# Blocks of normed rows transposed by VectorE and placed through memory, in a two-layer transformer kernel on one core

## The chip, the cores and the metric

The kernel runs on one core of a Trainium2 chip. The core has a matrix engine (TensorE, PE in the profile), a vector engine (VectorE, DVE), an activation engine (ScalarE, ACT), a general engine (GpSimd, POOL), an engine that mostly issues transfers (SyncE, SP), and 16 DMA engines that move data between the core's memory (SBUF) and device memory. Each engine runs its own instructions strictly in order and waits on semaphores for what other engines have still to deliver. The metric is the device time of one execution in microseconds (us): 2072.71 us, the median of three runs (2072.71, 2074.32 and 2067.70).

## What is computed

Two transformer layers on 4 × 512 tokens of 512 channels, in 32-bit floats. Cut to what matters here:

```python
x  = hidden_states                                  # 4 x 512 x 512
xn = layernorm(x)
x  = x + ttt_attention(xn) + ternary_ffn(xn)        # layer 0
xn = layernorm(x)
x  = x + latent_attention(xn) + moe_ffn(xn)         # layer 1

# ttt_attention: 32 heads of 16; per head a recurrence over 32 mini-batches of 16 tokens
Z1 = xk @ W1 + b1;  grad = fused_ln_l2_backward(Z1, xv - xk)
W1 = W1 - (eta * xk).T @ grad;  b1 = b1 - sum(eta * grad)
# ternary_ffn: silu(xn @ gate.T * gs) * (xn @ up.T * us) @ down.T * ds, inner size 1408
# latent_attention: c_kv = xn @ W_DKV + b, c_q = xn @ W_DQ + b, then 16 heads of 128
# moe_ffn: token g*4+e goes to expert e (fixed); silu(gate) * up @ down, inner size 512
```

What counts for the change is `xn`, twice. Layernorm is done with a token on each partition and its 512 channels along the free axis. The matmuls that use `xn` need it the other way round: a channel on each partition and tokens along the free axis. So each block of normed rows must be transposed.

## The kernel before

The first layer works in eight chunks of 256 tokens (`NCHUNK`, `CW`; 64 tokens of each of the four sequences). A chunk has two halves `u` of 128 rows. A loop over the 32 mini-batches issues the recurrence, which is a chain of short operations, and between its parts calls `fill(us)`. That draws work from a list of generators: the generator `between(ch)` yields, piece by piece with a cost estimate each, the products of the feed-forward net of chunk `ch` (`gate_up`, line 465, eleven times, then `down`, line 483), the transposition, keys, token rates and queries of chunk `ch + 1`, and `finish(ch - 1)`, which norms the recurrence's output, multiplies by `wo`, stores the layer's result to `yd` and norms it again for layer 1. At the end of `between(ch)` stands `norm_rows(ch + 2)`: loads of `x` and its layernorm. The order of each engine's instructions is made from this program order by the framework's scheduler; loads and stores of this stage are issued on SP (`nc.sync`), but for the last chunk's stores, which are on ScalarE's queue.

The rows are transposed in `transposed(src)` (line 144): four TensorE products with the identity, each turning 128 × 128, into one PSUM buffer from the two-buffer pool `pj`. For `x`, `norm_turn` copies the result to `xT` on ScalarE (line 157). `xT` holds 128 channels × 4 channel blocks × 256 tokens and is what `gate_up` and the key, value and query products read. For layer 1's rows (`x1`), `finish` copies it on ScalarE (line 603), tokens regrouped by expert (token index mod 4), to `xs` and stores that in device memory as `xe_d`, 256 KB for a half in 128 runs of 2 KB (line 604). The last two chunks keep the copy in SBUF too. In the last chunk's `between`, `latent_rows` loads chunks 0 to 5 of `xe_d` back, and `latents` (line 627) makes the latent projections `lat_d` from them. These are evicted from PSUM by VectorE and ScalarE in turn, in four operations for each projection, one for each sequence.

The mixture of experts follows (lines 899 to 1078). POOL issues the load of the first expert's gate weights `gu_0` (2 MB, line 924) and 14 loads of `xe` (line 928); SP issues the last two (through `fetch`). `xe` holds layer 1's rows as 128 channels × 16 halves × 4 channel blocks × 4 experts × 32 tokens. `tokens(e, c, h)` (line 940) takes expert `e`'s tokens from it: runs of 32 numbers. The experts' first product is done by Strassen's scheme: `right_sums` (line 944) forms four sums of token blocks, `t_ops`, on VectorE, and `left_sums` those of the weights, `s_ops`. Ahead of this stage, at line 833, POOL sets a 128 × 128 tile `ones` to 1; only the last product for the bias `bo`, in the attention stage, reads it. Its memory is reused from the first layer's stage.

The attention stage over 16 heads and four sequences comes last (lines 1084 to 1372). It already transposes its probabilities on VectorE in 32 × 32 blocks (line 1163) and places the blocks with 64 KB transfers on SP (line 1194).

Of the kernel before, what the change touches and what calls it, by code (L numbers as in the profile page):

```python
# [18 lines left out]
P = 128  # L19
# [36 lines left out]
def trunk_kernel(ctx: ExitStack, tc: tile.TileContext, a: dict, out: bass.AP):  # L56
# [12 lines left out]
    nc.vector.memset(eps_ln, LN_EPS)  # L69
    dram = ctx.enter_context(tc.tile_pool(name="dram", bufs=1, space=bass.MemoryType.DRAM))  # L70
    yd = dram.tile([B, L, HS], F32, tag="yd", name="yd")
    xe_d = dram.tile([2 * NCHUNK, P, NC, E, 32], F32, tag="xe_d", name="xe_d")
    lat_d = dram.tile([1 + QC // P, P, B, NCHUNK, CT], F32, tag="lat_d", name="lat_d")
    bo = const.tile([P, HS], F32, tag="bo", name="bo")

# [30 lines left out]
    with ExitStack() as px:  # L106
# [34 lines left out]
        def transposed(src):  # L141
# [2 lines left out]
                nc.tensor.transpose(pt[:, c, :], src[:, c * P : (c + 1) * P], ident)  # L144
            return pt

        def norm_rows(ch):
            for u in range(2):
                xt = wk.tile([P, HS], F32, tag="xt", name=f"xt{ch}_{u}", bufs=4)
                load_rows(xt, a["x"], ch, u)  # L150
                row_norm(xt, xt, f"{ch}_{u}")
                xns[ch, u] = xt

        def norm_turn(ch):
            xTs[ch] = wk.tile([P, NC, CW], F32, tag="xT", name=f"xT{ch}", bufs=3)
            for u in range(2):
                nc.scalar.copy(xTs[ch][:, :, u * P : (u + 1) * P], transposed(xns.pop((ch, u))))
                yield 0.6

        norm_rows(0)  # L160

# [69 lines left out]
        lrb_s = one.tile([P, NS, 4], F32, tag="lrb_s", name="lrb_s")  # L231
        nc.vector.tensor_copy(lrb_s, lrb[:, :P].rearrange("p (al r) -> p r al", r=32)[:, :NS, :])

        for _ in norm_turn(0):
            pass


        rows_d = [dram.tile([CH, NS, K, B, RW], F32, tag=f"rows{ch}", name=f"rows{ch}") for ch in range(NCHUNK)]
# [13 lines left out]
        def keys(ch):  # L252
            return features(ch, wk_w, k1, "k1", 2)
# [291 lines left out]
        def finish(ch):  # L545
            store = nc.sync if ch + 1 < NCHUNK else nc.scalar
            zb = zbs.pop(ch)
            sq = wk.tile([P, NC, CW], F32, tag="pn_sq", name=f"pn_sq_{ch}", bufs=1)
            nc.scalar.activation(sq, zb, AF.Square)
            for j in range(2):  # L550
                pv = psum()
                mm(pv, bones, sq[:, 2 * j : 2 * j + 2].rearrange("p c t -> p (c t)"))
                rs = wk.tile([P, 2, CW], F32, tag="pn_rs", name=f"pn_rs_{ch}_{j}", bufs=1)
                nc.scalar.activation(rs.rearrange("p c t -> p (c t)"), pv, AF.Sqrt, bias=eps_ttt, scale=1.0 / HD)
                for c in range(2):
                    be = 2 * j + c

                    tc.keep_in_program_order(nc.vector.reciprocal(rs[:, c], rs[:, c]))
                    nc.vector.scalar_tensor_tensor(
                        zb[:, be], zb[:, be], gamma_ch[:, be : be + 1], rs[:, c], ALU.mult, ALU.mult  # L560
                    )
            nc.vector.tensor_add(zb, zb, q1[ch])
            yield 1.72
            pm = psum()[:, :CW]
            mm(pm, onesd, over_blocks(sq, zb))

            for be in range(NC):
                nc.vector.scalar_tensor_tensor(
                    zb[:, be], zb[:, be], beta_ch[:, be : be + 1], pm, ALU.add, ALU.subtract
                )  # L570
            nc.scalar.activation(sq, zb, AF.Square)
            over_blocks(sq, sq)
            yield 0.43
            pt = psum()
            rt = wk.tile([P, 2], F32, tag="pn_rt", name=f"pn_rt_{ch}")
            for u in range(2):
                mm(pt[:, u : u + 1], sq[:, 0, u * P : (u + 1) * P], onesd[:, :1])
            nc.scalar.activation(rt, pt[:, :2], AF.Sqrt, bias=eps_ttt, scale=1.0)
            nc.vector.reciprocal(rt, rt)
            for u in range(2):  # L580
                po = psum()
                for be in range(NC):
                    mm(po, zb[:, be, u * P : (u + 1) * P], wo[:, be, :], be == 0, be == NC - 1)
                t = yf.pop((ch, u))
                nc.vector.scalar_tensor_tensor(t, po, rt[:, u : u + 1], t, ALU.mult, ALU.add)
                for b2 in range(2):
                    store.dma_start(
                        out=yd[2 * u + b2, ch * CT : (ch + 1) * CT, :], in_=t[b2 * CT : (b2 + 1) * CT, :]
                    )

                xt = wk.tile([P, HS], F32, tag="xt", name=f"x1_{ch}_{u}", bufs=4)
                row_norm(xt, t, f"1_{ch}_{u}")
                xns[ch, u] = xt
                yield 4.4
            if ch >= NCHUNK - 2:
                t = wk.tile([P, NC, CW], F32, tag="xT", name=f"xl_{ch}", bufs=3)
                part = parts[ch] = t.rearrange("p c w -> p (c w)").rearrange("p (u c e x) -> p u c e x", u=2, c=NC, e=E)
            for u in range(2):
                if ch >= NCHUNK - 2:
                    xs = part[:, u]  # L600
                else:
                    xs = wk.tile([P, NC, E, 32], F32, tag="xs", name=f"xs_{ch}_{u}", bufs=3)
                nc.scalar.copy(xs, transposed(xns.pop((ch, u))).rearrange("p c (j e) -> p c e j", e=E))
                store.dma_start(out=xe_d[2 * ch + u], in_=xs)
                yield 0.6


# [12 lines left out]
                lw.extend(t[:, :, i * P : (i + 1) * P] for i in range(n // P))  # L620

        def latent_rows(k):
            t = parts[2 * k, 2 * k + 1] = one.tile([P, 4, NC, E, 32], F32, tag=("wk", "wv", "wq")[k], name=f"xl_{k}")
            for i in range(4):
                nc.sync.dma_start(out=t[:, i], in_=xe_d[4 * k + i])

        def latents(key):

            part = parts.pop(key)
            ks = key if isinstance(key, tuple) else (key,)  # L630
            n = len(ks)
            for m, w in enumerate(lw):
                pl = psum()[:, : n * CW]
                for c in range(NC):
                    mm(pl, w[:, c, :], part[:, :, c], c == 0, c == NC - 1)
                st = wk.tile([P, 512], F32, tag="xs", name=f"lat_{ks[0]}_{m}", bufs=3)
                view = pl.rearrange("p (k u e b j) -> p k u e b j", k=n, u=2, e=E, b=2)
                to = st[:, : n * CW].rearrange("p (b k e j) -> p b k e j", b=B, k=n, e=E)
                for b in range(B):
                    part_b = view[:, :, b // 2, :, b % 2]  # L640
                    if m % 2:
                        nc.vector.tensor_scalar(to[:, b], part_b, lat_b[:, m : m + 1], None, ALU.add)
                    else:
                        nc.scalar.activation(to[:, b], part_b, AF.Identity, bias=lat_b[:, m : m + 1], scale=1.0)
                nc.scalar.dma_start(
                    out=lat_d[m][:, :, ks[0] : ks[0] + n], in_=to.rearrange("p b k e j -> p b k (e j)")
                )
                yield 1.72 * n

# [6 lines left out]
        def between(ch):  # L656

            fin = finish(ch - 1) if ch > 0 else iter(())
            if ch + 1 == NCHUNK:
                latent_operands()  # L660
            for i in range(NI):
# [6 lines left out]
                yield from finish_constants()  # L668
            nxt = iter(())
            if ch + 1 < NCHUNK:  # L670
                nxt = chain(
                    norm_turn(ch + 1), keys(ch + 1), token_tile(ch + 1, 0), token_tile(ch + 1, 1), queries(ch + 1)
                )
            else:
                yield from fin
            for u in range(2):
# [153 lines left out]
    buv = lat.tile([P, H], F32, tag="b_UV", name="b_UV")  # L830
    bo_part = lat.tile([P, HS], F32, tag="bo_part", name="bo_part")
    ones = lat.tile([P, P], F32, tag="ones", name="ones")
    nc.gpsimd.memset(ones, 1.0)
    ups = ["uk"] + [f"uq{i}" for i in range(QC // P)]

    def batch_latents(hg, b):
# [62 lines left out]
    with ExitStack() as px:  # L899
# [22 lines left out]

        gu = gate_w[0]
        nc.gpsimd.dma_start(out=gu, in_=a["gu"][0].rearrange("(c p) o -> p c o", p=P))
        xe = wg.tile([P, 2 * NCHUNK, NC, E, 32], F32, tag="xe", name="xe")
        for k in range(2 * NCHUNK):
            if k < 2 * NCHUNK - 2:
                nc.gpsimd.dma_start(out=xe[:, k], in_=xe_d[k])
            else:
                fetch(out=xe[:, k], in_=xe_d[k])  # L930
        ws = {0: gu, 1: gates(1)}
        dns = {0: downs(0)}

# [5 lines left out]

        def tokens(e, c, h):  # L940

            return xe[:, NCHUNK * h : NCHUNK * (h + 1), 2 * c : 2 * c + 2, e, :].rearrange("p k c j -> p c k j")

        def right_sums(e):
            t1, t2, t3, t4 = (t_ops[:, n].rearrange("p c (k j) -> p c k j", k=NCHUNK) for n in range(4))
            b22 = tokens(e, 1, 1)
            nc.vector.tensor_sub(t1, tokens(e, 0, 1), tokens(e, 0, 0))
            nc.vector.tensor_sub(t2, b22, t1)
            nc.vector.tensor_sub(t3, b22, tokens(e, 0, 1))
            nc.vector.tensor_sub(t4, tokens(e, 1, 0), t2)  # L950

        def left_sums(gu, i):

# [84 lines left out]
        right_sums(0)  # L1038
        for e in range(E):
            if e == 1:  # L1040
                nc.sync.dma_start(out=wqr, in_=a["W_QR"])
                nc.sync.dma_start(out=wkr, in_=a["W_KR"])
                buv16 = wk.tile([H, D], F32, tag="sg", name="buv16")
# [426 lines left out]
```

## Time and profile before

| | |
|---|---|
| median of three runs | 2072.71 us |
| lowest, highest | 2067.70, 2074.32 us |
| profiled execution | 2068.84 us |
| its span (first to last instruction) | 2067.1 us |
| mean TensorE clock granted in it | 0.988 |
| first layer's recurrence and products | about 40 to 981 us |
| mixture of experts | about 988 to 1165 us |
| attention stage | about 1165 to 2067 us |
| instructions in the trace | 30725 |
| DMA moved | 271.94 MB in 341254 packets |

A profile shows one execution. "Busy" is time in which an engine worked on an instruction; the rest is waiting. A row of the timeline or of the list of groups names engine, line, operation, output and inputs with their shapes; "x4" counts instructions, and brackets hold the time for which the engine stood idle just before and what ended that wait. A product of 32-bit floats leaves two records in the trace, a transposition through the identity one. Durations of products overlap, so the time that a sequence takes is read from the starts, not from the sum of durations.

### The profile page before, as it was taken

What the parts mean: (1) busy time and instruction counts of PE and PEld (TensorE: products, weight loads), DVE (VectorE), ACT (ScalarE), POOL (GpSimd) and SP (SyncE); (2) the same over time, 40 slices, a digit from 0 to 9 for tenths busy, and PEclk for the clock granted to TensorE, in tenths of its full rate; (3) what the DMA queues carried; (4) which work ended last, traced back from release to release, by engine and by line L of the source; (5) the groups of instructions that cost most, each with busy time, mean ns of one, the idle gap of its engine ahead of it and who ended that gap; (6) DMA issues with size and microseconds to landing.
All of it is one profiled execution on the core that took longest, in us unless ns stands there. A gap on an engine that the chain in (4) does not pass through costs nothing.

```text
span 2067.1 us, 30725 instructions
## 1 busy us (share of the span) xinstructions
PE 1983.4 (96%) x10486; PEld 1255.6 (61%) x10486; DVE 1302.3 (63%) x2722; ACT 866.2 (42%) x1763; POOL 587.5 (28%) x635
## 2 busy tenths in 40 slices
PE   8998999899999999998699999999999999999998
PEld 6776676767667776745577435555555555555554
DVE  5444667475755674744454487777777777777772
ACT  2233343333343443421122265555555555555552
POOL 5232333333332333311000222233223232354220
PEclk9999999999999999999899999999999999999999
DMA  6756566656464656643831144344444443433332
GB/s 164 205 141 181 136 190 158 173 144 178 115 186 126 161 168 170 198 127 122 286 107 57 48 112 118 96 109 109 107 98 110 106 107 87 109 86 95 96 92 83
DMA packets 341254, 271.94 MB, mean 132 GB/s; under 512 B 104299, under 2 KB 262188, under 8 KB 340460
## 3 DMA queue, kind: packets, MB, share of 16 engines
q1 hardware_dynamic: 326112, 255.41, 46.0%
q0 software_dynamic: 3488, 9.27, 1.4%
q10 hardware_dynamic: 11500, 5.32, 0.9%
q8 instruction: 84, 1.38, 0.3%
q14 instruction: 70, 0.57, 0.1%
HBM read 174.18 MB, written 34.87 MB: 101 GB/s over the span
## 4 chain that ended last, share of the span: by engine, by line
PE 46%; SPq 2%; DVE 2%; ACT 1%; DMA 1%; issue 0%; DVEq 0%; ACTq 0%
PE pc L1202 9%; PE sc L1134 9%; PE pq L1124 7%; PE px L1245 5%; PE p L1245 4%; PE epg L966 3%; PE epo L1029 3%; PE pk L1116 2%; SPq L1194 2%; PE epu L966 1%; PE po L1302 1%; PE pw L865 1%; PE pvo L883 1%; ACT prob L1139 1%; DVE tt L1163 0%
## 5 line engine op out<-in xcount | busy, mean ns | idle before, releaser
L1139 ACT ACTIVATE prob<-sc,mx 128x512 f32<-128x512 f32 x256 | 174.3, 683 | 157.6 <-DVE mx L1136 152.7
L1134 PE MATMUL sc<-kT,qT 96*128 96x512 f32 x512 | 230.9, 593 | 0.9 <-ACT prob L1139 0.6
L1202 PE MATMUL pc<-prT,lv 128*128 128x512 f32 x496 | 224.8, 596 | 3.7 <-DMA prT<-tt 3.7
L1163 DVE STREAM_TRANSPOSE tt<-prob 128x512 f32<-128x512 f32 x252 | 173.1, 706 | 56.0 <-ACT prob L1144 44.5
L1109 POOL TENSOR_TENSOR kT<-t_k,t_k 32x512 f32<-32x512 f32 x64 | 80.6, 1259 | 407.7 <-PE pq L1124 225.4
L117 PE MATMUL pf<-xT,wg 128*128 128x256 f32 x704 | 175.7, 392 | 12.5 <-DVE hid L478 6.8
L1144 ACT ACTIVATE prob<-prob,sm 128x512 f32<-128x512 f32 x256 | 176.3, 713 | 0.0
L1124 PE MATMUL pq<-cq,uq 128*128 128x512 f32 x384 | 175.3, 592 | 0.6 <-DVE t_k L1105 0.6
L117 PE MATMUL pf<-xT,wu 128*128 128x256 f32 x704 | 171.7, 388 | 1.6 <-DMA wu<-in_wu 1.6
L1134 PEld LDWEIGHTS sc<-kT,qT 96*128 96x128 f32 x512 | 96.7, 190 | 124.9 <-issue 120.1
L1136 DVE TENSOR_REDUCE mx<-sc 128x1 f32<-128x512 f32 x256 | 168.1, 677 | 5.8 <-PE sc L1134 3.8
L117 PE MATMUL pd<-wd,hid 128*128 128x512 f32 x352 | 165.3, 599 | 0.4 <-DMA wd<-in_wd 0.2
L117 PEld LDWEIGHTS pf<-xT,wg 128*128 128x128 f32 x704 | 133.5, 194 | 39.3 <-DVE hid L478 9.8
L1202 PEld LDWEIGHTS pc<-prT,lv 128*128 128x128 f32 x496 | 94.8, 191 | 99.4 <-issue 96.4
L117 PEld LDWEIGHTS pf<-xT,wu 128*128 128x128 f32 x704 | 137.4, 196 | 21.8 <-DMA wu<-in_wu 1.8
L478 DVE SCALAR_TENSOR_TENSOR hid<-pf,us,sg 128x256 f32<-128x256 f32 x88 | 41.8, 476 | 145.9 <-ACT sg L477 145.1
L1124 PEld LDWEIGHTS pq<-cq,uq 128*128 128x128 f32 x384 | 72.8, 190 | 92.8 <-issue 83.6
L314 POOL TENSOR_SCALAR sk<-k,m 128x256 f32<-128x256 f32 x64 | 61.0, 964 | 202.8 <-PE pz L117 189.6
L421 POOL TENSOR_SCALAR gh<-grad,m 128x256 f32<-128x256 f32 x64 | 62.3, 983 | 152.8 <-DVE grad L390 145.2
L117 PEld LDWEIGHTS pd<-wd,hid 128*128 128x128 f32 x352 | 63.6, 190 | 58.7 <-issue 44.6
L477 ACT ACTIVATE sg<-pf,gs 128x256 f32<-128x256 f32 x88 | 41.5, 473 | 135.1 <-PE pf L117 134.7
L1109 POOL TENSOR_TENSOR qT<-t_q,t_q 32x512 f32<-32x512 f32 x64 | 80.7, 1260 | 56.9 <-DVE t_q L1105 56.8
(295 smaller groups left out, 3503.9 us busy)
## 6 DMA issues: line engine op xcount, KB each, us to landing
prT<-tt SPq DMA_DIRECT2D x1008, 64.0 KB, 2.0
wd<-in_wd SPq DMA_DIRECT2D x176, 256.0 KB, 3.0
wg<-in_wg SPq DMA_DIRECT2D x88, 256.0 KB, 3.0
wu<-in_wu SPq DMA_DIRECT2D x88, 256.0 KB, 3.2
cq<-lat_d SPq DMA_DIRECT2D x48, 256.0 KB, 3.9
rows<-rows SPq DMA_DIRECT2D x128, 66.0 KB, 2.2
kv<-rows SPq DMA_DIRECT2D x32, 264.0 KB, 4.3
gu<-in_gu SPq DMA_DIRECT2D x3, 2048.0 KB, 7.9
```

The costliest lines, as they stand in the source:

```text
L117: nc.tensor.matmul(out, lhsT=lhsT, rhs=rhs, start=start, stop=stop, skip_group_check=True)
L421: nc.gpsimd.tensor_scalar_mul(gh[:, :, h, :], g, m2[:, h : h + 1])
L966: nc.tensor.matmul(ps, lhsT=w[:, c, :], rhs=x[:, c], start=start and c == 0, stop=c == 1, skip_group_check=True)
L1109: nc.gpsimd.tensor_sub(t[RD:mid, :], t1[RD:mid, :], t2[RD:mid, :])
L1124: nc.tensor.matmul(pq, lhsT=w[f"uq{i}"][:, h, :], rhs=cqs[hg, b][:, i, :], start=(i == 0), stop=(i == nq - 1))
L1134: pin(nc.tensor.matmul(ps, lhsT=qT[:KQ, i * P : (i + 1) * P], rhs=kT[:KQ, :], start=True, stop=True))
L1136: pin(nc.vector.tensor_reduce(mx, ps, AX.X, ALU.max, negate=True))
L1139: pin(nc.scalar.activation(pr, ps, AF.Exp, bias=mx, scale=1.0, accum_out=sm))
L1144: pin(nc.scalar.mul(pr, pr, sm))
L1163: nc.vector.transpose(out=tt[:, :, :, i, :], in_=pr.rearrange("p (kb e j) -> p kb e j", e=2, j=K))
L1202: pin(nc.tensor.matmul(pc, lhsT=lv[:, b, k, :], rhs=prT[:, k, :], start=(k == 0), stop=(k == E - 1)))
L1245: nc.tensor.matmul(ps[:, q, :], lhsT=a[:, k, q * P : (q + 1) * P], rhs=w[:, k, :], start=start and k == 0 and q == 0, stop=k == 1, skip_gr ...
```

## The change

Normed rows are transposed by VectorE, except those of chunk 0 of `x` and of chunks 6 and 7 of `x1`. `nc.vector.transpose` on 128 × 512 turns each 32 × 32 block in place within its 32 partitions. The new `turned_out` then writes the tile to device memory with four stores on SP, one for each group of 32 partitions, 32 rows × 16 blocks × 128 bytes (64 KB), so that the blocks come to stand where a full transpose has them. For `x` it writes to the new `x_d[ch]` at the end of `norm_rows`; `norm_turn` is then one load of `xT` (512 KB, runs of 1 KB), at the start of `between(ch)` for chunk `ch + 1`, and no longer a pair of pieces among its work. For `x1` it writes `xe_d` in `finish`, right after the norm; the expert order within a block of 32 tokens comes from the write pattern of the VectorE operation.

`xe_d` has a new layout: per half 16 blocks × 32 channels × 4 token groups × 32 tokens. All its loads go through `by_channel`, which gives runs of 512 bytes. So expert `e`'s tokens in `xe` come in runs of eight numbers; `tokens` is changed to that, and `right_sums` works in eight operations of 256 columns instead of four of 512. The evictions of the latents go by chunk and half row instead of by sequence. The setting of `ones` moves from line 833, ahead of POOL's loads of the mixture of experts, to the second expert's turn.

```diff
-    xe_d = dram.tile([2 * NCHUNK, P, NC, E, 32], F32, tag="xe_d", name="xe_d")
+    xe_d = dram.tile([2 * NCHUNK, 4 * NC, 32, 4, 32], F32, tag="xe_d", name="xe_d")
+    def by_channel(blocks):
+        return blocks.rearrange("(c q) r t x -> (q r) c (t x)", q=4)
...
+        x_d = [dram.tile([4 * NC, 32, 8, 32], F32, tag=f"x{ch}", name=f"x{ch}") for ch in range(NCHUNK)]
+        def turned_out(dst, src, k, nm, es):
+            t = wk.tile([P, 4 * NC, es, 32 // es], F32, tag="xs", name=f"xs_{nm}", bufs=3)
+            nc.vector.transpose(
+                out=t.rearrange("p b e j -> p b j e"), in_=src.rearrange("p (b j e) -> p b j e", j=32 // es, e=es)
+            )
+            for q, r in enumerate(quarters):
+                nc.sync.dma_start(
+                    out=dst[:, :, k + q, :].rearrange("b r x -> r b x"), in_=t[r].rearrange("p b e j -> p b (e j)")
+                )
         def norm_rows(ch):
...
                 row_norm(xt, xt, f"{ch}_{u}")
-                xns[ch, u] = xt
+                if ch == 0:
+                    xns[ch, u] = xt
+                else:
+                    turned_out(x_d[ch], xt, 4 * u, f"{ch}_{u}", 1)
         def norm_turn(ch):
             xTs[ch] = wk.tile([P, NC, CW], F32, tag="xT", name=f"xT{ch}", bufs=3)
+            if ch > 0:
+                nc.sync.dma_start(out=xTs[ch], in_=by_channel(x_d[ch]))
+                return
...
                 row_norm(xt, t, f"1_{ch}_{u}")
-                xns[ch, u] = xt
+                if ch < NCHUNK - 2:
+                    turned_out(xe_d[2 * ch + u], xt, 0, f"1_{ch}_{u}", E)
+                else:
+                    xns[ch, u] = xt
                 yield 4.4
+            if ch < NCHUNK - 2:
+                return
...
             for u in range(2):
-                if ch >= NCHUNK - 2:
-                    xs = part[:, u]
-                else:
-                    xs = wk.tile([P, NC, E, 32], F32, tag="xs", name=f"xs_{ch}_{u}", bufs=3)
-                nc.scalar.copy(xs, transposed(xns.pop((ch, u))).rearrange("p c (j e) -> p c e j", e=E))
-                store.dma_start(out=xe_d[2 * ch + u], in_=xs)
+                nc.scalar.copy(
+                    part[:, u].rearrange("p c (q e j) -> p c q e j", q=4, e=E),
+                    transposed(xns.pop((ch, u))).rearrange("p c (q j e) -> p c q e j", q=4, e=E),
+                )
+                store.dma_start(out=by_channel(xe_d[2 * ch + u]), in_=part[:, u])
...
-                for b in range(B):
-                    part_b = view[:, :, b // 2, :, b % 2]
+                for k in range(n):
+                    for h in range(2):
...
         def between(ch):
             fin = finish(ch - 1) if ch > 0 else iter(())
+            if ch + 1 < NCHUNK:
+                norm_turn(ch + 1)
...
-                    norm_turn(ch + 1), keys(ch + 1), token_tile(ch + 1, 0), token_tile(ch + 1, 1), queries(ch + 1)
+                nxt = chain(keys(ch + 1), token_tile(ch + 1, 0), token_tile(ch + 1, 1), queries(ch + 1))
...
-    nc.gpsimd.memset(ones, 1.0)
...
-                nc.gpsimd.dma_start(out=xe[:, k], in_=xe_d[k])
+                nc.gpsimd.dma_start(out=xe[:, k], in_=by_channel(xe_d[k]))
...
         def tokens(e, c, h):
-            return xe[:, NCHUNK * h : NCHUNK * (h + 1), 2 * c : 2 * c + 2, e, :].rearrange("p k c j -> p c k j")
+            part = xe[:, NCHUNK * h : NCHUNK * (h + 1), 2 * c : 2 * c + 2]
+            return part.rearrange("p k c (q e j) -> p c k q e j", q=4, e=E)[:, :, :, :, e]
         def right_sums(e):
-            t1, t2, t3, t4 = (t_ops[:, n].rearrange("p c (k j) -> p c k j", k=NCHUNK) for n in range(4))
+            for c in range(2):
+                t1, t2, t3, t4 = (t_ops[:, n, c].rearrange("p (k q j) -> p k q j", k=NCHUNK, q=4) for n in range(4))
...
             if e == 1:
+                nc.gpsimd.memset(ones, 1.0)
```

## The prediction

> **What bounds the kernel now.** I began with the page's engine line and slices, then read the shares of fixed stretches, the tiles the change touches, and the border between the first layer and the MoE stage as a timeline.
>
> ```profile
> PE 1983.4 (96%) x10486; PEld 1255.6 (61%) x10486; DVE 1302.3 (63%) x2722; ACT 866.2 (42%) x1763; POOL 587.5 (28%) x635
> PE   8998999899999999998699999999999999999998
> ```
>
> TensorE is busy 96% of the span and every other engine has room, VectorE (63%) included. The slices show one dip, the "8 6" of slices 19 and 20 (930 to 1033 us), at the border. So two things pay: a matmul taken off TensorE, and that dip. The stretches (columns: window, length, then busy us and count of PE, PEld, DVE, ACT, POOL, then granted clock, DMA share, GB/s) say the same:
>
> ```profile
> 700.00:750.00 50.00, 50.00 (x454) 41.56 (x453) 22.29 (x57) 19.34 (x35) 18.43 (x26) 1.00 0.66 179
> 950.00:1000.00 50.00, 33.32 (x116) 23.21 (x116) 14.48 (x45) 7.47 (x26) 8.52 (x16) 0.88 0.71 254
> ```
>
> In the recurrence TensorE is full, VectorE under half busy, and the 16 DMA engines already two thirds busy. Across the border TensorE loses 17 of 50 us. The answer for the transposes' line 144, and the timelines of TensorE and POOL there:
>
> ```profile
> L144 PE MATMUL pj<-ident,xt x64: 272/273/446, 8.8 to 759.3; 128*128 128x128 f32 x64
> L144 PE MATMUL pj<-ident,x x64: 272/273/329, 236.7 to 969.1; 128*128 128x128 f32 x64
> ...
>   POOL ones L833: 62.0, 1
> ```
>
> ```profile
> 967.54 0.60 PE L144 MATMUL pj<-ident,x 128*128 128x128 f32 x4
> ...
> 973.91 7.28 PE L117 MATMUL pj<-xl,W_DQ 128*128 128x256 f32 x32
> 988.15 5.29 PE L966 MATMUL epg<-xe,gu 128*128 128x256 f32 x16 [6.96 <-DMA xe<-xe_d]
> 1000.82 2.93 PE L966 MATMUL epu<-t_ops,s_ops 128*128 128x256 f32 x6 [7.38 <-DVE t_ops L947]
> ```
>
> ```profile
> 968.20 0.20 POOL L833 MEMSET ones<- 128x128 f32 x1 [62.05 <-PE pj L144]
> 968.92 0.83 POOL L924 DMA_DIRECT2D gu<-in_gu  x1 [0.52 <-ACT lat L644]
> ```
>
> The setting of `ones` waits 62 us for the last transposes, because its memory was an `xt`. POOL runs in order, so the load of `gu_0` (2 MB) and fourteen loads of `xe` stand behind it until 968.9. TensorE then waits 6.96 us for `xe`, and 7.38 us for `t_ops`.
>
> **Transposes leave TensorE.** Of 32 halves, 26 go: four transposes and a copy each. Four take 0.60 us as a group, of which the last one's 0.27 overlaps what follows: 0.33 for three steps, 0.11 each, 0.43 us per half. 26 × 0.43 = **-11 us**, as TensorE is full there; -8 if some fell into gaps, -13 if waits beside them go too. ScalarE loses 26 copies of 0.585 us (15 us), covered. VectorE gains 26 transposes; the attention stage shows that form:
>
> ```profile
> L1163 DVE STREAM_TRANSPOSE tt<-prob 128x512 f32<-128x512 f32 x252 | 173.1, 706 | 56.0 <-ACT prob L1144 44.5
> ```
>
> 26 × 0.706 = 18 us on an engine idle more than half of each stretch: nothing on the path. Without that cover a step of the recurrence would wait 0.7 us, 18 at most.
>
> A rule speaks against this: the Trainium skill, "VectorE: DVE Perf Modes", section "Rules for kernel authors", says to transpose 128×128 on TensorE where PSUM will do as destination. By the rule 0.43 us becomes 0.71 and transfers on top, a loss of 26 × 0.28 = 7 us. The rows agree on the durations, but TensorE's microsecond is on the path and VectorE's isn't, so I keep -11.
>
> **Transfers that place the blocks.** Each half becomes four SP stores of 64 KB in 128 B runs: 104 stores, seven loads of `xT` (512 KB, 1 KB runs), less 12 stores of 256 KB. The same form is in the trace, the reordering of weights:
>
> ```profile
> L86 SPq DMA_DIRECT2D blocks_d<-in_W_UQ x48: 490/513/1277, 107.1 to 410.9; - x48
> ...
> SPq L471 <- PE pf L117: 225.4, 147, 11.6
> SPq L489 <- PE pd L117: 126.7, 125, 11.0
> ```
>
> SP's issue: (104 + 7 - 12) × 0.51 = 50 us over 940. SP has that time: the last two rows (its waits before 985 us) show it waiting 352 us for weight buffers. But it works in order. A half's stores wait for VectorE's transpose, and behind them stand weight loads (`wg`, `wu`, `wd`) and the `z` stores; `xT`'s load waits for the stores to land (2.7 us), though it is issued most of a chunk (some 115 us) ahead of its use, so what it delays is only the queue behind it. A weight load lands in 3.0 us, and its buffer comes free one `gate_up` (5.2 us) ahead of use: 2.2 us of slack. Four issues are 2.0 us; a wait on VectorE on top breaks the slack. Chunks 3 to 7 have a weight load behind such stores; each costs 0 to 5 us. In their favour the order before also put `rows` and `z` stores, with waits up to 8.7 and 14.6 us, ahead of weights.
>
> The rule against it: "DMA: Bandwidth & Descriptors", section "Rules for kernel authors", wants small transfers joined, since under 64 KB it is mostly overhead; its "Specifications" put line rate at 512 B runs and up. From 220 to 232 us, almost all such runs, 2616 packets held 29.1% of 16 engines: 12 × 16 × 0.291 / 2616 = 21 ns each. 53,248 packets × 21 ns / 16 = 70 us, 7 to 8% more share on some 60%. By the rule alone I'd count the 70 us as loss; the landing (2.7 us against 2.5 for the 256 KB store) says one store isn't slow, and the share stays under three quarters. Queue and share together: **+6 us**, ends 0 and +35.
>
> **The border.** `ones` is set only in expert 1, behind POOL's loads; its one reader is the last product for `bo`, some 1000 us later, so the move itself costs nothing. These now wait for the last down product and VectorE's work for chunk 7's output, around 948 by the old clock: 20 us earlier. 5.5 MB (2 MB and 14 × 256 KB) then land before TensorE needs them, and both waits go (6.96 + 7.38), except what is late next: VectorE's eight sums of gate weights (0.34 us steps) and `t_ops`, about 1.3 us after TensorE arrives. -13. Two things give some back. TensorE's order now has chunk 6's latents ahead of chunk 7's norm sums, so fewer products lie between the sums and what they wait for: an estimated +4 us, from the waits in the tail now (2.88, 1.64, 1.23 us and smaller ones). And `lat_d`'s stores may meet the early loads, as those of 128 KB did before (11.0 us against 2.6). **-9 us**, ends -14 and 0.
>
> **Edits with one answer.** `right_sums` in eight operations of 256 (0.42 us) in place of four of 512 (0.68): +0.6 us the first time, then hidden. The latents' evictions are two of 128 for four of 64: below 0.5. `tokens` reads runs of 8 numbers instead of 32. TensorE in this trace reads 16-number runs (`wh`) as fast as whole ones (219 ns both), so 0; if it slowed, 96 products with tokens as moving operand × 0.43 us pitch bound it at +41. `xe` loads in 512 B runs: 14 × 1536 more packets × 21 ns / 16 = 28 us of engines if packets stay as dear, before it is needed.
>
> **Sum:** -11 + 6 - 9 + 0.6 = -13.4 on 2068.84 (span 2067.1 and 1.7 around it) = 2055.4. The median of the runs shown, 2072.71, is 3.9 higher; the same difference gives **2059**.
>
> **Rivals.**
> - *Both gains come whole.* SP's stores slip between waits it has anyway (352 us): -11 - 13 = -24, 2049 by the median. For it: SP's idle time. Against: the order of its queue. 0.20.
> - *Nothing is left.* Weight loads late by 3 to 4 us per chunk eat it: +20, 2073, within 0.3% (6.2 us, about what runs can tell from no change). 0.13.
> - *SP's order decides.* Stores waiting for VectorE hold weight loads in all groups: 26 × 1.3 us = 34, so 2087. It beats the gains from 0.8 us per half. For it: TensorE already waits 5.6 us for `wg` in two places, and DMA is at 0.66; against: SP's waits end before TensorE's need in most chunks. 0.24.
> - *Token reads slow:* -13.4 + 41, 2100. 0.05.
> - *The border stays*, since another wait holds POOL: -11 + 6 + 0.6, so 2068; part of the second's 0.13.
>
> My forecast has 0.38, its own range 2050 to 2066. Faster 0.58, same 0.13, slower 0.29. The 8-in-10 range leaves the token case and the ends of the first and third out: 2041 to 2088.
>
> **What would show it.** TensorE's transposes down from 128 to 24; no wait over 2 us for `xe` or `t_ops`; POOL's `gu_0` load some 20 us before the last transposes; TensorE's waits for `wg`, `wu`, `wd` at 10 us or less in the first layer (over 30 means SP's order); L966's matmul at 379 ns still. I am wrong if the waits for weights grow by more than 20 us, or if the tail before the MoE stage opens gaps beyond 10.

## The result

The changed kernel takes **2114.64 us** (median of four runs, 2110.05 to 2117.20) against 2070.20 us before (2065.21 to 2074.32): a ratio of 1.0224, 95% interval 1.0203 to 1.0244. It is slower, by some 46 us by that ratio.

The page of the changed kernel, the same lines as those shown of before:

```profile
PE 1989.7 (94%) x10382; PEld 1253.8 (59%) x10382; DVE 1322.8 (63%) x2756; ACT 851.6 (40%) x1728; POOL 591.9 (28%) x635
PE   8999989898979979999879999999999999999998
```

104 TensorE records are gone (10486 to 10382), and yet TensorE is busy for 6 us *more*, in a span longer by 46.3 us (2113.4). The slices show where: single 7s and 8s in the middle of the first layer. The border to the mixture of experts, first TensorE and then SP, shows what was forecast and something that wasn't:

```profile
1027.18 5.72 PE L122 MATMUL pj<-xl,W_DQ 128*128 128x256 f32 x24
1032.74 3.62 PE L995 MATMUL epg<-xe,gu 128*128 128x256 f32 x16
1036.86 0.70 PE L995 MATMUL epu<-t_ops,s_ops 128*128 128x256 f32 x2 [0.50 <-DVE t_ops L976]
...
1071.21 2.08 PE L995 MATMUL epu<-xe,s_ops 128*128 128x256 f32 x4 [13.17 <-ACT hold L1031]
```

The two waits at the border (6.96 and 7.38 us) are down to 0.50. But TensorE stands 13.17 us a little later, with 104 of the 112 product records of expert 0 behind it. The row names ScalarE's `hold`, and the chain goes on from there: `hold` waits for VectorE's `inter`, which stands behind a transposition of attention weights, `wt`, and that waits for a load, `raw`. VectorE, ScalarE, then SP:

```profile
1069.41 0.71 DVE L897 STREAM_TRANSPOSE wt<-raw 128x512 f32<-128x512 f32 x1 [13.49 <-DMA raw<-blocks_d]
1070.79 0.37 ACT L1031 COPY hold<-epu 128x256 f32<-128x256 f32 x1 [13.95 <-DVE inter L1044]
```

```profile
1036.07 0.37 SPq L938 DMA_DIRECT2D gu<-in_gu  x1
1036.49 0.50 SPq L938 DMA_DIRECT2D dn<-in_dn  x1
1037.04 2.43 SPq L938 DMA_DIRECT2D y<-yd  x4
...
1063.74 2.34 SPq L903 DMA_DIRECT2D raw<-blocks_d  x1
```

So `raw` stands in SP's queue behind 7 MB: the second expert's gate weights `gu_1`, the first's down weights `dn`, and `y`. In between SP waits in turn for the landing of `gu_1` (2.2 us), of `dn` (2.3) and of one `y` after another (2.1 to 2.8), that is, each transfer for the one eight places ahead of it. The DMA engines are 96% busy from 1036 to 1058 us. In the kernel before, these loads began at 981 us, and the waits for `xe` and `t_ops` covered them:

```profile
1022.91 0.71 DVE L870 STREAM_TRANSPOSE wt<-raw 128x512 f32<-128x512 f32 x1 [2.83 <-DMA raw<-blocks_d]
```

The last latent product ends at 1032.9 instead of 981.2: **the first layer is longer by 51.7 us**, and that is the loss. TensorE's waits from 40 us on, name, total, times and longest, of the changed kernel:

```profile
PE pf L122 <- DVE hid L500: 28.7, 8, 5.5
PE pf L122 <- DMA wg<-in_wg: 18.3, 7, 6.1
PE pso L122 <- POOL gh L443: 13.6, 9, 3.0
```

and of the kernel before:

```profile
PE pso L117 <- POOL gh L421: 8.8, 3, 5.9
PE pf L117 <- DVE hid L478: 6.8, 4, 3.9
PE pf L117 <- DMA wg<-in_wg: 5.6, 2, 4.0
```

One place shows both large waits, at the start of a chunk. TensorE and then SP:

```profile
491.89 0.70 PE L122 MATMUL pz<-gsum,bones 128*128 128x256 f32 x2
493.32 1.08 PE L122 MATMUL pz<-wq_bd,sk 128*32 128x128 f32 x32 [0.72 <-ACT wq_bd L354]
494.21 0.63 PE L122 MATMUL pso<-wq_bd,wh 128*32 128x64 f32 x32
494.77 2.86 PE L122 MATMUL pd<-wd,hid 128*128 128x512 f32 x6
503.08 3.78 PE L122 MATMUL pf<-xT,wg 128*128 128x256 f32 x8 [5.45 <-DVE hid L500]
506.66 3.11 PE L122 MATMUL pf<-xT,wu 128*128 128x256 f32 x8
509.60 1.89 PE L122 MATMUL pf<-xT,wg 128*128 128x256 f32 x8
511.32 1.89 PE L122 MATMUL pf<-xT,wu 128*128 128x256 f32 x8
515.93 3.65 PE L122 MATMUL pf<-xT,wg 128*128 128x256 f32 x8 [2.72 <-DMA wg<-in_wg]
```

```profile
502.62 5.50 SPq L161 DMA_DIRECT2D x<-xs  x8
508.17 0.51 SPq L476 DMA_DIRECT2D z<-zch  x1
509.75 0.38 SPq L178 DMA_DIRECT2D xT<-x  x1
510.18 2.26 SPq L476 DMA_DIRECT2D z<-zch  x2
512.49 0.49 SPq L493 DMA_DIRECT2D wg<-in_wg  x1
```

The wait of 2.72 us is a weight load that stood in SP's queue behind eight stores of `x`, the `z` stores and `xT`. The wait of 5.45 us is another thing. The last down products of the chunk (`pd`) come *behind* the next chunk's first recurrence product (`pz`). At the same chunk of the kernel before they came ahead of it:

```profile
483.92 1.88 PE L117 MATMUL pd<-wd,hid 128*128 128x512 f32 x4
...
492.84 0.59 PE L117 MATMUL pz<-gsum,bones 128*128 128x256 f32 x2
```

In the changed kernel VectorE works through the recurrence's step first (from 494.46 us), then the norm of one half of `x` and the start of the other's, the eviction of `pd` (`yf`) and a transposition, and only then frees a buffer of `pf` by writing the next chunk's `hid`:

```profile
501.29 0.69 DVE L516 TENSOR_TENSOR yf<-pd,dsc 128x512 f32<-128x512 f32 x1
501.89 0.70 DVE L157 STREAM_TRANSPOSE xs<-xt 128x512 f32<-128x512 f32 x1
502.52 0.14 DVE L140 BATCH_NORM_AGGREGATE ln_mv<-ln_st 128x2 f32<-128x6 f32 x1
502.58 0.45 DVE L500 SCALAR_TENSOR_TENSOR hid<-pf,us,sg 128x256 f32<-128x256 f32 x1
```

With both of the `pf` buffers full TensorE can't go on.

### The profile page after: what moved, and what is told of

Same layout as the page of the kernel before. It is cut to its first block, busy times and chain, and to the rows that moved or that the text cites. A ratio compares the mean times of both kernels' runs of the same rounds, so it can differ in the third digit from the quotient of the medians.

```text
span 2113.4 us, 30686 instructions
## 1 busy us (share of the span) xinstructions
PE 1989.7 (94%) x10382; PEld 1253.8 (59%) x10382; DVE 1322.8 (63%) x2756; ACT 851.6 (40%) x1728; POOL 591.9 (28%) x635
## 4 chain that ended last, share of the span: by engine, by line
PE 47%; DMA 1%; DVE 1%; SPq 1%; ACT 1%; issue 0%; ACTq 0%; DVEq 0%
PE pc L1232 10%; PE sc L1164 10%; PE pq L1154 8%; PE px L1275 5%; PE p L1275 4%; PE epo L1058 3%; PE epg L995 3%; PE pk L1146 3%; PE epu L995 1%; DMA y<-yd 1%; PE po L1332 1%; PE pw L892 1%; PE pvo L910 1%; SPq L1224 0%; ACT prob L1169 0%; DMA raw<-blocks_d 0%
## 5 line engine op out<-in xcount | busy, mean ns | idle before, releaser
L122 PE MATMUL pf<-xT,wg 128*128 128x256 f32 x704 | 187.3, 410 | 47.8 <-DVE hid L500 28.7
L1193 DVE STREAM_TRANSPOSE tt<-prob 128x512 f32<-128x512 f32 x252 | 173.0, 705 | 55.8 <-ACT prob L1174 43.2
L122 PEld LDWEIGHTS pf<-xT,wg 128*128 128x128 f32 x704 | 139.9, 204 | 84.5 <-DVE hid L500 37.1
L343 POOL TENSOR_SCALAR km<-kv,m2n 128x256 f32<-128x256 f32 x64 | 63.5, 1005 | 162.8 <-DMA kv<-rows 149.7
```

The lines of the kernel that those rows point to most:

```text
L122: nc.tensor.matmul(out, lhsT=lhsT, rhs=rhs, start=start, stop=stop, skip_group_check=True)
L343: nc.gpsimd.tensor_scalar_mul(km[:, :, :, h, :], kv[:, :, 0:64].rearrange("p b (al d) -> p b al d", d=HD), m2n[:, h : h + 1])
L1193: nc.vector.transpose(out=tt[:, :, :, i, :], in_=pr.rearrange("p (kb e j) -> p kb e j", e=2, j=K))
```

## The experiments

Three theories: **Q**, SP's queue holds weight loads behind the new transfers; **V**, VectorE's transpositions hold the evictions; **P**, packets of 128 bytes crowd the DMA engines. A fourth, **Pace**, came after the first eight runs. Each kernel ran against the kernel before on the same chip, with ratios as given; the median of before lies between 2067.5 and 2069.8 us in these runs.

**x alone.** The x1 rows go back to TensorE:

```diff
-                if ch < NCHUNK - 2:
-                    turned_out(xe_d[2 * ch + u], xt, 0, f"1_{ch}_{u}", E)
-                else:
-                    xns[ch, u] = xt
+                xns[ch, u] = xt
```

> Only the rows of x are turned by VectorE and placed through memory; the x1 rows go by TensorE and one store a half, in the new layout of xe_d. Theory Q/V (the x part sits where the next chunk starts: its eight stores and the xT load stand in SP's queue ahead of that chunk's weight loads, and its norms and transposes stand in VectorE's queue ahead of the evictions of hid): nearly the whole loss stays, 2100 to 2115 us. Theory P (packets of 128 B crowd the 16 DMA engines, wherever they come from): 56 of 104 stores are left, so about half of the loss, 2085 to 2095 us.

Measured: 2127.52 us, 1.0294 (1.0275 to 1.0313), some 13 us above the whole change. TensorE waits 60.2 us for `wg`, in six waits of up to 16.2.

**x1 alone.** x goes by TensorE as before, with its pieces in `between`:

```diff
-                if ch == 0:
-                    xns[ch, u] = xt
-                else:
-                    turned_out(x_d[ch], xt, 4 * u, f"{ch}_{u}", 1)
+                xns[ch, u] = xt
```

> Only the x1 rows are turned by VectorE; x goes by TensorE as before. Q/V: the loss is gone but for what stays at the border (gu_1 late), 2060 to 2080 us. P: 48 of 104 stores are left, so 2085 to 2095 us.

Measured: 2082.65 us, 1.0075 (1.0057 to 1.0094). Waits for `wg` 11.8 us, for `hid` 10.2. The larger loss comes with x, as Q and V said, but x1 isn't free.

**ones alone.** The kernel before with the setting of `ones` moved:

```diff
-    nc.gpsimd.memset(ones, 1.0)
...
             if e == 1:
+                nc.gpsimd.memset(ones, 1.0)
```

> The kernel before with only the setting of ones moved to the second expert. If POOL's loads were held by it alone, the waits for xe and t_ops (7.0 and 7.4 us) shrink: 2056 to 2065 us, TensorE's order unchanged up to the mixture of experts. If another wait holds POOL at nearly the same time: 2068 to 2072.

Measured: 2060.93 us, 0.9966 (0.9954 to 0.9978), some 7 us faster. The order of TensorE, VectorE, ScalarE and SP in the first layer is that of before. The two waits went nearly whole, and most of the gain was lost again in the next one, within expert 0. VectorE's row shows that it is `raw` here too:

```profile
983.08 1.56 PE L965 MATMUL epu<-t_ops,s_ops 128*128 128x256 f32 x6 [0.96 <-DVE t_ops L946]
...
1014.81 2.08 PE L965 MATMUL epg<-t_ops,s_ops 128*128 128x256 f32 x4 [12.01 <-ACT hold L997]
```

```profile
1012.81 0.71 DVE L869 STREAM_TRANSPOSE wt<-raw 128x512 f32<-128x512 f32 x1 [12.54 <-DMA raw<-blocks_d]
```

**Long runs.** The stores write the tile as it lies, in runs of 2 KB; this leaves out the placement of the blocks, so the kernel's result is not the layer's:

```diff
-                    out=dst[:, :, k + q, :].rearrange("b r x -> r b x"), in_=t[r].rearrange("p b e j -> p b (e j)")
+                    out=flat(dst, k)[r], in_=t[r].rearrange("p b e j -> p (b e j)")
```

> The changed kernel, with each of the 104 stores writing 32 runs of 2 KB (the tile as it lies) instead of 512 runs of 128 B; bytes, instructions and waits are the same, the placement of the blocks is left out. P: the loss goes, 2060 to 2080 us. Q/V: it stays, 2105 to 2115 us, for the queues hold the same instructions in the same places.

Measured: 2108.92 us, 1.0210 (1.0185 to 1.0235). The interval overlaps that of the change itself. P is out as the main cause: with stores in runs sixteen times as long the loss stays where it was.

**ScalarE's queue.** The x stores and the `xT` loads are issued by `nc.scalar`:

```diff
-                nc.sync.dma_start(
+                eng.dma_start(
...
-                nc.sync.dma_start(out=xTs[ch], in_=by_channel(x_d[ch]))
+                nc.scalar.dma_start(out=xTs[ch], in_=by_channel(x_d[ch]))
```

> The changed kernel, with the x stores and the xT loads issued on ScalarE's queue instead of SP's; x1's stores stay on SP. Q (SP's queue holds the weight loads): TensorE's waits for wg fall from 18 us (60 in the run with x alone) below 8, and the time to 2065 to 2090 us, if ScalarE isn't held in turn. V (VectorE's order holds the evictions of hid): waits for wg shrink but those for hid stay near 29 us, 2095 to 2115 us.

Measured: 2111.80 us, 1.0198 (1.0174 to 1.0222): no change that the intervals tell, and the waits for `wg` stay at 18.5 us. Of SP's waits in this run:

```profile
SPq L493 <- DMA x<-xs: 20.4, 4, 8.5
SPq L493 <- DMA xT<-x: 10.4, 2, 5.3
```

The weight loads (line 493) on SP wait for the stores and loads on ScalarE. So a transfer of SP waits for others ahead of it (in the rows at 1036 us above, for the one eight places ahead) across the two queues as well. This run did not take the dependence away, then, and doesn't speak against Q.

**Transpositions nobody reads.** The kernel with only `ones` moved, and besides:

```diff
                 xns[ch, u] = xt
+                if ch > 0:
+                    spare = wk.tile([P, HS], F32, tag="xs", name=f"spare_{ch}_{u}", bufs=3)
+                    nc.vector.transpose(out=spare, in_=xt)
```

> The kernel with only ones moved, and besides a VectorE transposition of each x half into a spare tile that nothing reads: VectorE's 14 operations alone, without stores or loads. V: the evictions of hid come later, 2070 to 2090 us. Q: nothing but 10 us of covered work on VectorE, 2058 to 2066 us.

Measured: 2064.55 us, 0.9975 (0.9967 to 0.9983); `hid` waits 6.3 us. The interval overlaps that of `ones` alone. In the order of before VectorE had room for these 14, so the transpositions alone don't make the loss. In the changed kernel's order V isn't excluded: there a transposition stands directly ahead of `hid` (the rows at 501.89 and 502.58 us).

**Late stores.** The x stores are kept back, and issued after two later `gate_up`s; `xT`'s load follows:

```diff
                 yield from gate_up(ch, i)
+                if i in (3, 5) and pending:
+                    pending.pop(0)()
+                if i == 7 and 0 < ch < NCHUNK - 1:
+                    norm_turn(ch + 1)
```

> The changed kernel, with the x stores taken out of norm_rows and issued later in the program, after the fourth and sixth gate_up of the next chunk, and the xT load after the eighth: the same instructions and packets, but weight loads come ahead of them in SP's queue. Q: the waits for wg go, 2065 to 2090 us (what x1 alone gave is 2083). V: 2100 to 2115 us.

Measured: 2092.93 us, 1.0110 (1.0091 to 1.0129): some 22 us of the loss gone, with the same instructions and packets. The waits for `wg` no longer stand among the larger ones; those for `hid` stay:

```profile
PE pf L122 <- DVE hid L509: 29.8, 6, 5.5
```

Q is shown for a part. Since idle transpositions alone don't make the `hid` waits, what does? The order of TensorE's products, as in the rows at 491 to 503 us above. And what makes that order is the bookkeeping of `fill`: with the turns, four pieces of 0.6 a chunk (two of `x`, two of `x1`) went out of the work list.

**gu_1 early.** `ones` alone, with `gu_1`'s load ahead of the last two of `xe`, and the pools of this stage in another order in memory so that `gu_1` lies on no latents. The run was made in the belief that TensorE's 12 us are a wait for `gu_1`, as were those further down that name it:

```diff
-        one = px.enter_context(tc.tile_pool(name="d_one", bufs=1, reuse_waits="tile"))
         wd = px.enter_context(tc.tile_pool(name="d_wd", bufs=2, reuse_waits="tile"))
         wg = px.enter_context(tc.tile_pool(name="d_wg", bufs=1, reuse_waits="tile"))
+        one = px.enter_context(tc.tile_pool(name="d_one", bufs=1, reuse_waits="tile"))
...
+        gu_1 = gates(1)
         xe = wg.tile([P, 2 * NCHUNK, NC, E, 32], F32, tag="xe", name="xe")
```

> The kernel with only ones moved, and besides the pools of the mixture of experts in another order in memory and gu_1's load ahead of the last two of xe, so that gu_1 waits for nothing of the latents. If the 12 us that TensorE stands before expert 1 in the run with ones alone are the late gu_1: 2046 to 2053 us. If something else holds it there: 2058 to 2064 us.

Measured: 2058.47 us, 0.9947 (0.9927 to 0.9968): the second expectation, something else holds TensorE there. The interval overlaps that of `ones` alone. `gu_1` is asked for at 973.6 us instead of 978.7, but `raw` is there no earlier than in the run with `ones` alone:

```profile
1014.88 0.71 DVE L869 STREAM_TRANSPOSE wt<-raw 128x512 f32<-128x512 f32 x1 [6.76 <-DMA raw<-blocks_d]
```

TensorE's wait is 6.2 us instead of 12.0 because TensorE came there later, after 3.8 us of waiting for `t_ops` and a later start of expert 0. In twelve of the kernels here, the one before included, TensorE goes on 1.8 to 2.0 us after this transposition starts. Asking for `raw` itself earlier wasn't tried.

**Pace.** The changed kernel, with empty pieces where the turns had stood:

```diff
-                nxt = chain(keys(ch + 1), token_tile(ch + 1, 0), token_tile(ch + 1, 1), queries(ch + 1))
+                nxt = chain(iter((0.6, 0.6)), keys(ch + 1), token_tile(ch + 1, 0), token_tile(ch + 1, 1), queries(ch + 1))
...
             if ch < NCHUNK - 2:
+                yield 0.6
+                yield 0.6
                 return
```

> The changed kernel, with only the pacing of before restored: two empty pieces of 0.6 where the x turns stood in the chain of between, and two at the end of finish for chunks 0 to 5. No instruction is added or removed. Pace (a third theory: without those pieces fill hands out the rest of a chunk so that its last down product comes behind the next chunk's first recurrence product; the evictions of hid stand in VectorE's order behind the result of that down product, and TensorE waits for PSUM): waits for hid fall from 29 to under 10 us, 2070 to 2095 us. V (VectorE's transpositions and norms as such): 2105 to 2115. Q alone: waits for wg stay near 18 us.

Measured: 2125.34 us, 1.0276 (1.0255 to 1.0298). The `hid` waits fall from 28.7 to 12.4 us as Pace said, but the time rises: waits for weights grow to 47 us. One of them, first TensorE, then SP:

```profile
409.43 3.78 PE L122 MATMUL pf<-xT,wg 128*128 128x256 f32 x8 [17.94 <-DMA wg<-in_wg]
```

```profile
398.54 4.13 SPq L161 DMA_DIRECT2D x<-xs  x8
...
404.21 0.38 SPq L178 DMA_DIRECT2D xT<-x  x1
...
405.19 0.48 SPq L493 DMA_DIRECT2D wg<-in_wg  x1
```

This is Q at full size. The stores of `x` wait until 398.5 for VectorE, which has the recurrence's step ahead of the norm; then come the stores, the rest of `z`, `xT` and only then a weight load, which lands 4 us later. In the changed kernel the down products, put late, fill a part of that hole (2.86 us at 494.77 us above).

**Late stores and pace together.** Both edits of above.

> Late x stores and the pacing of before together. If Pace and Q are the whole loss in the first layer: waits for hid and wg together under 15 us, 2060 to 2075 us, with the 13 us before expert 1 (late gu_1) still in it. If the transfers cost something beside: 2080 us or more.

Measured: 2074.67 us, 1.0033 (1.0022 to 1.0045); `wg` 6.7 and `hid` 2.9 us. So the four kernels make a square:

| ratio to before | stores early | stores late |
|---|---|---|
| pieces gone | 1.0224 (the change) | 1.0110 |
| pieces kept | 1.0276 | 1.0033 |

By these ratios late stores are worth 50 us with the pieces kept and 24 with them gone. The pieces are worth 16 us with late stores, and cost 11 with early ones. The two causes cover each other, so neither shows its size alone. A new row leads the waits here, the squares of `finish`, and the wait in expert 0 is still there (12.9 us):

```profile
PE pj L122 <- ACT pn_sq L580: 19.6, 5, 6.3
```

**The same with gu_1 early** (the edit of above, pools in an order that suits this layout).

> As the run before, and gu_1 loaded ahead of the last two of xe with the pools of the mixture of experts placed so that it waits for no latents. The wait before expert 1 goes: 6 to 12 us less than late stores with pacing, 2050 to 2066 us.

Measured: 2070.14 us, 1.0010 (0.9997 to 1.0023), 4.5 us less than without, with intervals that just overlap; not below 2066. The wait in expert 0 is 5.1 us, with 2.8 before `t_ops`, and VectorE has `raw` 2.5 us earlier than without.

**The kernel before without its pieces.** TensorE turns everything, as before, the halves of `x` now at the start of `between`:

```diff
-                nxt = chain(
-                    norm_turn(ch + 1), keys(ch + 1), token_tile(ch + 1, 0), token_tile(ch + 1, 1), queries(ch + 1)
-                )
+                nxt = chain(keys(ch + 1), token_tile(ch + 1, 0), token_tile(ch + 1, 1), queries(ch + 1))
...
+            if ch + 1 < NCHUNK:
+                norm_turn(ch + 1)
...
                 store.dma_start(out=xe_d[2 * ch + u], in_=xs)
-                yield 0.6
+                if ch >= NCHUNK - 2:
+                    yield 0.6
```

> The kernel before, transposing on TensorE as it did, but with the x turns issued at the start of between without pieces of their own, and without the two pieces at the end of finish for chunks 0 to 5, as in the changed kernel. No VectorE transposition, no new transfer. Pace: TensorE waits for hid by 20 to 30 us, 2085 to 2110 us. Q or V: 2066 to 2076 us.

Measured: 2092.28 us, 1.0115 (1.0087 to 1.0144): 25 us lost with no new transfer and no VectorE transposition. The down products again come behind the recurrence's first product. The waits are spread otherwise than expected: `gh` 18.8 us (8.8 before), `hid` 11.6. At the chunk shown above the wait for `hid` is 2.49 us, not 5.45: less of the norm and no transposition stands ahead of `hid` on VectorE, which comes from the recurrence's first operation to `hid` in 5.1 us instead of 8.1. So a part of the changed kernel's `hid` waits (28.7 us) is VectorE's new work, in this order; what it costs in time no run separates.

**x late and paced, x1 on TensorE.** The edits of late stores and pace for `x`, that of x alone for `x1`.

> Only x turned by VectorE, stores late, pacing of before kept; x1 on TensorE with its pieces. If x is free once order and pacing are mended: 56 transpositions less than in the run with ones alone, 6 us, so 2052 to 2062 us. If x still costs (transfers, VectorE): 2066 to 2078 us.

Measured: 2058.41 us, 0.9952 (0.9935 to 0.9968). x costs nothing once its stores are late and its pieces kept; whether it gains the 6 us of its 56 transpositions over `ones` alone (0.9966) the intervals don't tell.

**x1 paced, x on TensorE.** The edit of x1 alone, with two empty pieces of 0.6 at the end of `finish`.

> Only x1 turned by VectorE, with two empty pieces of 0.6 at the end of finish for chunks 0 to 5; x on TensorE. If x1's 22 us came from the pacing: 2058 to 2066 us. If they come from its stores in SP's queue (ahead of weight loads and z) or the later latents: 2074 to 2086 us.

Measured: 2071.23 us, 1.0020 (1.0012 to 1.0029): between the two expectations. The pieces were 11 of x1's 22 us (against `ones` alone). Most of the rest has a row, 15.2 us of waits for `pn_sq` where `ones` alone has 4.9; why the squares of `finish` come later with x1's stores in the queue wasn't tried.

**x late and paced, with gu_1 early.**

> x late and paced, x1 on TensorE, with gu_1 early and the pools placed as in the last run of late stores with pacing and gu_1. If the gains add: 2046 to 2056 us, below the 2058 of ones and gu_1 alone.

Measured: **2051.95 us**, 0.9920 (0.9902 to 0.9939), below both kernels of the comparison. Its interval overlaps that of `gu_1` early alone, and just overlaps that of `x` late and paced without `gu_1` early: VectorE has `raw` at 1006.9 us, against 1007.7. The wait in expert 0 is 7.4 us.

## Why the prediction was wrong

It forecast 2059 us, faster; 2114.6 lies above its range. By its steps:

- **Transposes leave TensorE, -11.** The records are gone (128 to 24). The same step said that this stage's TensorE is full and that nothing else moves with them. *That is the first step that failed.* The turns were also four pieces of 0.6 in the list by which the kernel deals out its work, and taking them out moved the down products behind the next recurrence step. The step counted what the pieces do, not what they hold in place: 25 us with the pieces gone from the kernel before, 16 in the changed kernel with the stores late.
- **VectorE, 0.** Right in the order of before, where 14 idle transpositions left the time within the intervals. Not shown in the new order, where one stands ahead of `hid`: the forecast took the engine's idle share for room at each place. Those of x took 0.702 us as expected, those of x1, which write in expert order, 1.076.
- **Transfers, +6 (0 to +35).** *The second that failed, in its size.* The mechanism was named, with the queue and what stands in it, but a chunk was priced at 0 to 5 us from the weights' slack of 2.2. The price is how long the stores wait for VectorE, and that is a whole recurrence step: waits of 7 to 18 us a chunk in the runs with x alone and with pieces kept, 50 us between early and late stores. In the changed kernel the weight waits are 21.8 us in all (`wg` 18.3, `wd` 2.2, `wu` 1.3), between the marks of 10 and 30 that were to tell right from wrong. The rival "SP's order decides", at 1.3 us a half, was the right kind; against the square's 50 us it was too small as well.
- **DMA share.** Too high, in the cautious direction: the queue's share of the first layer went from 54.7 to 55.8%, and the stores landed in 2.0 us (1.7 with long runs, at no gain in time that the intervals show). So the rule on small transfers, weighed for this step, decided nothing here. The loads of gate and up weights did land later, in 3.8 us instead of 3.0 and 3.2; with long runs it was 3.7, and with late stores and pace 2.9 and 3.1.
- **The border, -9.** *The third that failed.* The two waits went (14.3 to 0.5 us), POOL's first load came 19.4 us ahead of the last transposes, and the tail gave back 4.2 us of gaps where 4 was forecast. But "what is late next" was looked for up to `t_ops` only. The two waits had covered SP's 7 MB of loads; without them VectorE stood for `raw`, and TensorE behind it for 13.2 us (waits for `hold` were 3.3 before): net -3, and with the tail's gaps nothing; `ones` alone brought -7. That it is `raw` is read from the rows, and `gu_1` asked for earlier didn't take the wait away; an earlier request for `raw` itself was not tried.
- **Edits with one answer.** `tokens` cost nothing (379 ns, as before), `right_sums` 0.42 us each.

The sum misses one more term. The first layer is 51.7 us longer; TensorE's waits there, summed from its timeline, grew by 45 (from 43 to 88), less 11 for the transposes: 18 remain. They are in the rows at 503 to 516 us. Eight products take 1.89 us at 511.32; after the wait of 5.45 us the same eight took 3.78, and after one of 2.72 us 3.65. Read from the starts, the first of these waits cost 3.1 us beyond itself and the second 1.8 (the products after it start at 519.42). A stretch with such waits says the same as granted clock (0.90):

```profile
600.00:650.00 50.00, 38.23 (x249) 27.72 (x247) 24.70 (x58) 13.53 (x26) 16.23 (x20) 0.90 0.62 173
```

Summed over the first layer in stretches of 4 us, what the granted clock lacked of 1, times TensorE's busy time, is 12 us before and 30 after. These 18 more are an estimate (15 with stretches of 10 us), and they are the size of what remains.

The Trainium skill, "TensorE: Matmul & The Clock Gate", section "Why this matters for your kernels", has the rule: no gap above about 3 us between bursts, or the clock falls to half. The half is in the rows (and the granted clock is 0.50 from 503 to 508 us), the 3 us are not. In the kernel before eight products took 2.72 us after a wait of 2.00, and in the changed kernel 1.97 after one of 2.96:

```profile
505.58 2.72 PE L117 MATMUL pf<-xT,wg 128*128 128x256 f32 x8 [2.00 <-DVE hid L478]
```

```profile
394.59 1.97 PE L122 MATMUL pf<-xT,wg 128*128 128x256 f32 x8 [2.96 <-DMA wg<-in_wg]
```

So a wait of 2 to 3 us may cost itself alone or as much again, and the longer one above cost 3 us more. The prediction left this out of every wait it priced.

## What to carry to other kernels

Where an order written out by hand or by a budget deals out the work, a piece that is removed must leave its place in the budget, or be checked for what then comes ahead of what; a cost of "less work" alone isn't the price. A store that waits for a compute engine is priced by the longest thing ahead of it on that engine, not by its own issue, and belongs behind the loads that others wait for. When a wait at a border is removed, ask what it had covered: follow each engine's order past the first user, and a wait that names one engine through to the load behind it.

## What was not expected of the hardware

TensorE's products ran at half rate after a wait of 2.72 us (3.65 us for eight, 1.89 in stride) and slower than in stride after one of 2.00 (2.72), but not after one of 2.96 (1.97): the length of the wait alone doesn't decide. A VectorE transposition of 128x512 takes 0.702 us when it writes runs and 1.076 when its output steps by the expert order.
